# Load order, edge coefficients, late weights and pool waits in a fused grid, attention and MLP kernel

## The chip, the cores and the metric

The kernel runs on one core of a Trainium2 chip. The metric is device time in microseconds (us) of one execution; three runs are given and their median counts. The engines are TensorE (PE; its weight loads are PEld), VectorE (DVE), ScalarE (ACT), GpSimd (POOL) and SyncE (SP). SP only issues DMAs and reads registers. ACT and POOL issue DMAs as well; a DMA of SP or ACT is on a hardware queue, one of POOL on a software queue, and all of them use the same 16 DMA engines.

## The reference

The input x is (8, 512, 512) in f32. Four layers follow one another:

```python
# L0: one explicit step on a 512 x 512 grid, for each of the 8 batches
df = -(grad(A0*f, 1) + grad(A1*f, 2)) + 0.5*(grad2(B0*f, 1) + grad2(B1*f, 2)
      + grad(grad(B2*f, 2), 1) + grad(grad(B2*f, 1), 2))
x = maximum(f + df * dt, 0)             # one-sided differences in the outermost rows and columns
# L1: attention block with 16 heads, and an MLP
emb = silu(sin_emb(timestep)) @ W_ada + b_ada ; scale, shift = split(emb)
x = layernorm(x) * (1 + scale) + shift
q, k, v = x @ Wq + bq, x @ Wk + bk, x @ Wv + bv
probs = softmax(where(mask, -inf, q @ k.T / sqrt(32) + bias))
x = x + (probs @ v) @ Wo + bo
x = x + gelu2((layernorm(x) * g2 + beta2) @ W1 + b1) @ W2 + b2
# L2: an expert MLP chosen by an index per batch
x = layernorm(gelu(x @ Wi[e] + bi[e]) @ Wo_e[e] + bo[e] + x) * gamma[e] + beta[e]
# L3: a gated low-rank response
x = x + sigmoid(gate(mean(x))) * sigmoid(safety) * (x @ basis @ basis.T @ resp.T + resp_b + safety_bias)
```

The attention bias is (8, 16, 512, 512) in f32, 128 MB; it is the largest input. All matmuls are in f32.

## The kernel before

Three stages stand in the program one behind the other. `grid_stage` does L0 for batch 0 only, builds the grid's coefficient arrays and writes them to DRAM; I call it the front. `attention_stage` walks over 128 units (batch, group of four heads, quarter of the rows) and does the attention; in its gaps it also does the grid step of the next batches, from the coefficients in DRAM. `mlp_stage` does the two MLPs and L3, sixteen passes with the same matmul scheme. Nearly every instruction is pinned (`pin`, `tc.keep_in_program_order`), so each engine works through its list in the order of the program text. An instruction in the list that waits holds up all that is behind it on its engine; for SP and ACT this holds for DMA issues too. The hardware DMAs take eight completion semaphores in turn, POOL's DMAs eight others; a DMA may have to wait until the earlier one with the same semaphore has landed. I call this a slot wait.

**The embedding** (L104 to L139). ACT issues loads of ti (the time steps), freq, bada, sigs (the safety scores), eidx (the expert numbers), and later gw, dth, g2, beta2 and b1. DVE turns ti and freq into an angle ang; ACT takes Sin, Silu and, for sigs, Sigmoid, each with a table load of 1.28 us. This small work stands ahead of the front's large work on DVE. `embed` (L148) is 32 matmuls of 8 columns, each in two passes, into pe; `embed_out` (L157) adds bada and gives ada.

**The front's loads** (SP, L274). b1 and a1 in halves, b0, a0, the grid f, b2, 1 MB each as a whole; then wada in two halves of 1 MB, Wq, Wk, Wv, Wo (1 MB each), the rows of bq, bk, bv, and bo.

**The front's stencil.** DVE forms ca, cb, cc, ce, cg by sums of the raw arrays (ACT scales cc and b2), and then products with f: e, g, c, ga, gb, q, t. PE adds these up with shift matrices (L243), 28 matmuls of 512 columns in two passes each, into four PSUM banks acc. DVE forms x from acc row by row (L240), ACT takes the ReLU (L486).

**The edge rows.** Rows 0 and 511 of all batches need one-sided differences. They are done for all 8 batches together on 64 partitions: fe holds the edge rows of x, ec twelve coefficient rows, the same for every batch. POOL loads both behind an instruction gate_e that waits for f: for each of four column blocks one DMA of fe, and two of ec that read each DRAM row eight times. Some 23 DVE instructions (from qe on) make xe. Four DMAs of two pieces of 512 bytes put batch 0's edge rows from xe into x, two by SP and two by ACT (L492). POOL writes xe to DRAM as xed (L479), for the other batches.

**The coefficient writes.** Behind an instruction gate_c that waits for q, POOL issues writes of b2, ce, cc, cg, ca, cb to DRAM (coef_q, e, c, g, a, b; 1 MB each, and a few single rows).

**The front's end.** Statistics of x's rows (L499, L500), a power on POOL (L508), the scaling (L511), `embed_out`, and then in the attention stage the transposes xtr of x (`x1_in`) with scale and shift, pq and pk (the matmuls with Wq and Wk for the first head group), qt and kt, their evacuations by DVE and ACT, and the scores s. SP meanwhile reads the eight expert numbers from eidx (L1267), and then loads, in this order, mask mu, the grid gf of batch 1 (seven DMAs), gq (two halves of coef_q), the bias bt of unit 0, one half of coef_e (into xt of batch 1) and of coef_c, mask 1, the bias of unit 1, gg (half of coef_g), the bias of unit 2, and so on. POOL adds the mask to the bias (L950).

**Pools.** Each stage opens pools of tiles, and a new stage's tiles lie in memory that an older pool has given back. Without an option, the first use of such a tile waits until everything in the memory given back has been finished.

Of the kernel before, what the change touches and what calls it, by code (L numbers as in the profile page):

```python
# [11 lines left out]
F32 = mybir.dt.float32  # L12
# [8 lines left out]
NB = 8  # L21
# [18 lines left out]
def fused_kernel(ctx: ExitStack, tc: tile.TileContext, a: dict):  # L40
# [65 lines left out]
    nc.scalar.dma_start(freq, a["c_freq"])  # L106
    bada = ep.tile([P, 2 * KC], F32, name="bada")
    nc.scalar.dma_start(bada, a["b_ada"])
    nc.scalar.dma_start(sigs, a["safety"][None, :].to_broadcast([P, NB]))
    nc.scalar.dma_start(eidx, a["eidx"][None, :])  # L110
    nc.vector.tensor_scalar(bada[:, 0:KC], bada[:, 0:KC], 1.0, None, ALU.add)
# [27 lines left out]
    nc.scalar.activation(sigs, sigs, AF.Sigmoid)  # L139
# [14 lines left out]

    def embed_out(pe):
        tc.keep_in_program_order(
            nc.vector.tensor_tensor(  # L157
                ada, pe, bada[:, :, None].to_broadcast([P, 2 * KC, NB]), ALU.add
            )
        )  # L160
# [4 lines left out]
    def load_w():  # L165
        for n in ("Wq", "Wk", "Wv", "Wo"):
            w[n] = w8(wo8, n)
            nc.sync.dma_start(w[n], a[n].rearrange("(k p) m -> p k m", p=P))
# [5 lines left out]
    def load_rows():  # L174
        nc.sync.dma_start(bqk[:, 0, :], a["bq"])
# [6 lines left out]
        embed_out,  # L182
# [3 lines left out]
    io = ctx.enter_context(tc.tile_pool(name="io", bufs=1))  # L186
    g2 = const.tile([P, 2, KC], F32, name="g2")
    nc.scalar.dma_start(g2[:, 0, :], a["g2"])
    nc.scalar.dma_start(g2[:, 1, :], a["beta2"])
    b1 = const.tile([P, NJ], F32, name="b1")  # L190
    nc.scalar.dma_start(b1, a["b1"])
# [4 lines left out]
        g2, mhalf,  # L196
# [18 lines left out]
def grid_stage(  # L215
    tc, a, const, small, dram, x, mhalf, ident, load_wada, load_w, load_rows, embed,
    embed_out,
# [27 lines left out]
    with ExitStack() as ctx:  # L245
# [22 lines left out]
        pin(nc.gpsimd.memset(ec, 0.0))  # L268
# [7 lines left out]
        with tc.tile_pool(name="raw", bufs=1) as rp:  # L276
# [4 lines left out]
            def edge_in(i, k):  # L281
                lo, hi = max(0, W * k - 1), min(D, W * k + W + 1)
                u = slice(lo - W * k + 1, hi - W * k + 1)
                p0 = n * i
                pin(nc.gpsimd.dma_start(fe[p0 : p0 + n, :, u], a["edge_f"][:, :, lo:hi]))
                for side in range(2):
                    p1 = p0 + side * NB
                    pin(
                        nc.gpsimd.dma_start(
                            ec[p1 : p1 + NB, :, u],  # L290
                            a["edge_c"][side : side + 1, :, lo:hi].to_broadcast([NB, 12, hi - lo]),
                        )
                    )
# [9 lines left out]
            nc.scalar.dma_start(gw, a["c_ghost"].to_broadcast([P, 16]))  # L303
            nc.scalar.dma_start(dth, a["dt"][None, :].to_broadcast([P, NB]))
            load_wada()
            load_w()
# [6 lines left out]
            for i, k in enumerate(blocks):  # L313
                edge_in(i, k)
# [11 lines left out]
        wp = ctx.enter_context(tc.tile_pool(name="l0", bufs=1))  # L326
# [54 lines left out]
        for m, w, o in (  # L381
            ("q", b2, 1), ("e", ce, 1), ("c", cc, 0), ("g", cg, 1), ("a", ca, 0), ("b", cb, 0)
# [94 lines left out]
        xed = dram.tile([n, D], F32, name="xed")  # L477
        for i, k in enumerate(blocks):
            pin(nc.gpsimd.dma_start(xed[:, W * k : W * k + W], xe[n * i : n * i + n, :]))  # L479
        pe = embed(ps)  # L480
        pin(nc.vector.tensor_scalar(dth, dth, 0.5, None, ALU.mult))
        st = small.tile([P, R, 6], F32, name="ln0_st", tag="ln0_st", bufs=1)
        mv = small.tile([P, R, 2], F32, name="ln0_mv", tag="ln0_mv", bufs=1)
        for r in (0, 3, 1, 2):
            stt(x[:, r, :], acc[r], dth[:, 0:1], f[:, r, :], ALU.mult, ALU.add)
            pin(nc.scalar.activation(x[:, r, :], x[:, r, :], AF.Relu))  # L486
        for o, u, c in ((0, 3 * n, 0), (n, n, 2 * W)):
            for side, q_ in ((0, nc.sync), (1, nc.scalar)):
                p, r = side * (P - 1), side * (R - 1)
                e0 = o + side * NB  # L490
                pin(
                    q_.dma_start(  # L492
# [1331 lines left out]
```

## Time and profile before

| | us |
|---|---|
| runs (three) | 2828.27, 2830.43, 2831.24; median 2830.43 |
| profiled execution | 2828.87 |
| its span, first to last instruction | 2826.4 |
| PE busy | 2731.6 (97%) |
| DVE busy | 1942.6 (69%) |
| POOL busy | 1502.6 (53%) |
| ACT busy | 1003.3 (35%) |
| mean granted TensorE clock | 0.989 |
| chain that ended last, share of PE | 81% |

The page gives shares of the whole span; the front is some 70 us of it. Inside the front the timeline is the view to read: for each run of instructions its start, its length, engine, line, operation and tiles, and in brackets how long the engine had been idle and what released it. "SPq" and "ACTq" rows are DMA issues; a long one is an issue that was held up. The stretches table gives for each interval the busy time of each engine, the granted clock, and the share and rate of the DMA engines.

A few more rows of the front that the change touches, as start and length in us: the memset of ec on POOL 0.95, 1.39; the Sigmoid table load on ACT 7.70, 1.28; the first large DVE addition (ca) 11.05, 1.22; e on DVE 24.12, 2.29; the first stencil matmul on PE 26.51; fe and ec issues on POOL from 24.09 to 34.4, with 7.1 to 8.7 from issue to landing; qe on DVE 43.05, with 1.42 idle before it, for ec; xe's last instruction 51.82; gate_c on POOL 38.16; coef_b issued at 49.51 with 14.2 to landing; qt on DVE 77.06; gq on DVE from 77.72 (two in 4.28); the first softmax instruction on DVE 88.28.

### The profile page before, as it was taken

The page shows a single profiled execution, that of the slowest core. Times are in us where ns is not written, and L with a number is a line of the kernel's source. Part 1 is how long each engine was busy: PE and PEld are TensorE (multiplying, and loading weights), DVE is VectorE, ACT ScalarE, POOL GpSimd, SP SyncE. Part 2 cuts the span into 40 slices and gives each one's busy share as a digit, 9 for nine tenths or more (in the row PEclk, how much of TensorE's full clock was granted, in tenths as well). Part 3 has the DMA queues.
Part 4 walks back from the last instruction along what each step waited for, and adds up shares of the span by engine and source line. Part 5 has one row for each costly group of instructions (what it writes and reads, how often), then busy time and mean ns, then how long its engine had stood idle before and what let it go on. Part 6 is the DMA issues. An engine that isn't in the chain of part 4 may idle for free.

```text
span 2826.4 us, 39775 instructions
## 1 busy us (share of the span) xinstructions
PE 2731.6 (97%) x14646; PEld 2013.2 (71%) x14646; DVE 1942.6 (69%) x3583; ACT 1003.3 (35%) x2133; POOL 1502.6 (53%) x1080
## 2 busy tenths in 40 slices
PE   5999999999999998999999999999999999999997
PEld 3455555555555554888888888887888888888885
DVE  6889898888888766576756666655466565556654
ACT  1466666666666666211211211111121121121120
POOL 3455555555555553566555656564455455445532
PEclk9999999999999999999999999999999999999998
DMA  9665757666665554642444253343224233133110
GB/s 303 220 211 173 235 176 239 203 210 215 190 228 187 162 156 144 190 125 71 120 140 123 51 157 123 80 122 123 98 68 138 78 105 124 63 131 112 45 71 30
DMA packets 190399, 405.60 MB, mean 144 GB/s; under 512 B 24104, under 2 KB 28784, under 8 KB 183934
## 3 DMA queue, kind: packets, MB, share of 16 engines
q1 hardware_dynamic: 185192, 391.93, 41.8%
q0 software_dynamic: 3680, 11.07, 3.1%
q8 instruction: 116, 1.90, 0.3%
q14 instruction: 77, 0.63, 0.1%
q10 hardware_dynamic: 1334, 0.07, 0.0%
HBM read 367.32 MB, written 31.50 MB: 141 GB/s over the span
## 4 chain that ended last, share of the span: by engine, by line
PE 81%; DVE 13%; ACT 2%; issue 1%; POOL 0%; DVEq 0%; POOLq 0%; ACTq 0%
PE u L1137 27%; PE y L1137 24%; PE tr L546 6%; PE s L543 4%; PE ctx L543 4%; PE o L543 3%; PE pv L543 3%; PE pq L543 3%; PE pk L543 2%; DVE bt L973 2%; DVE tb L1143 2%; DVE x L663 1%; DVE pt L998 1%; ACT bt L978 1%; DVE act L1143 1%
## 5 line engine op out<-in xcount | busy, mean ns | idle before, releaser
L1137 PE MATMUL y<-wo,act 128*128 128x256 f32 x2560 | 578.9, 381 | 0.0
L950 POOL TENSOR_TENSOR bt<-bt,mk 128x1024 f32<-128x1024 f32 x256 | 543.2, 2143 | 63.8 <-DMA bt<-in_bias 62.9
L1137 PEld LDWEIGHTS y<-wo,act 128*128 128x128 f32 x2560 | 479.3, 190 | 82.2 <-issue 20.5
L978 ACT ACTIVATE bt<-bt,mn 128x512 f32<-128x512 f32 x512 | 365.5, 715 | 116.3 <-DVE mn L973 116.2
L546 PEld LDWEIGHTS tr<-ident,bt 128*128 128x128 f32 x2048 | 228.1, 141 | 168.8 <-issue 115.5
L1137 PE MATMUL u<-bt,wi 128*128 128x256 f32 x1440 | 332.4, 381 | 0.0
L973 DVE CUSTOM_DVE_ANT_0 bt<-s,bt 128x512 f32<-128x512 f32 x512 | 330.4, 683 | 0.0
L1143 DVE TENSOR_TENSOR act<-u,u 128x512 f32<-128x512 f32 x256 | 173.4, 687 | 212.8 <-PE u L1137 138.0
L1137 PEld LDWEIGHTS u<-bt,wi 128*128 128x128 f32 x1440 | 274.6, 191 | 37.6
L546 PE MATMUL tr<-ident,bt 128*128 128x128 f32 x2048 | 280.0, 278 | 19.3 <-DVE pt L998 8.1
L998 DVE COPY pt<-tr 128x512 f32<-128x512 f32 x256 | 175.9, 687 | 110.6 <-PE tr L546 110.3
L1137 PE MATMUL u<-tb,ws 128*128 128x256 f32 x1024 | 242.3, 379 | 0.0
L1137 PE MATMUL y<-t,s 128*128 128x256 f32 x1024 | 234.1, 380 | 0.0
L1137 PEld LDWEIGHTS u<-tb,ws 128*128 128x128 f32 x1024 | 195.0, 190 | 26.7
L1000 ACT COPY pt<-tr 128x512 f32<-128x512 f32 x256 | 148.3, 579 | 180.1 <-PE tr L546 177.7
L1146 POOL TENSOR_TENSOR t<-wo,t 128x512 f32<-128x512 f32 x64 | 104.6, 1650 | 198.2 <-PE y L1137 198.2
L1137 PEld LDWEIGHTS y<-t,s 128*128 128x128 f32 x1024 | 190.6, 190 | 23.8
L1143 DVE TENSOR_TENSOR x<-y,x 128x512 f32<-128x512 f32 x96 | 64.6, 686 | 182.5 <-PE y L1137 128.5
L1449 ACT ACTIVATE act<-act,bi 128x512 f32<-128x512 f32 x128 | 83.9, 712 | 292.2 <-DVE act L1143 292.1
L1449 ACT ACTIVATE act<-act,b 128x512 f32<-128x512 f32 x128 | 82.9, 712 | 292.5 <-DVE act L1143 292.5
L543 PE MATMUL s<-kt,qt 32*128 32x512 f32 x1024 | 170.8, 643 | 2.1 <-DVE mn L973 1.1
L1143 DVE TENSOR_TENSOR u<-u,u 128x512 f32<-128x512 f32 x192 | 131.3, 684 | 59.5 <-PE u L1137 59.5
(313 smaller groups left out, 4282.4 us busy)
## 6 DMA issues: line engine op xcount, KB each, us to landing
bt<-in_bias SPq DMA_DIRECT2D x256, 512.0 KB
wo<-in_W SPq DMA_DIRECT2D x32, 1024.0 KB
wi<-in_Wi SPq DMA_DIRECT2D x32, 1024.0 KB
wo<-in_Wo_e SPq DMA_DIRECT2D x32, 1024.0 KB
wi<-in_W SPq DMA_DIRECT2D x28, 1024.0 KB
gq<-coef_q SPq DMA_DIRECT2D x21, 512.0 KB
x1d<-x SPq DMA_DIRECT2D x8, 1024.0 KB
x<-x1d SPq DMA_DIRECT2D x8, 1024.0 KB
```

Of the source, the lines that this page charges most:

```text
L543: pin(nc.tensor.matmul(out, lhsT=lhsT, rhs=rhs, start=start, stop=stop))
L546: pin(nc.tensor.transpose(out, src, ident))
L663: pin(nc.vector.tensor_tensor(out, x, y, op))
L950: nc.gpsimd.tensor_tensor(bt, bt, mask[b, r][:, None, :].to_broadcast([P, 2, S]), ALU.add)
L973: nc.vector.tensor_tensor_reduce(bt[:, i, :], ss[h], bt[:, i, :], -1.0, 3.0e38, ALU.add, ALU.min, mn)
L978: nc.scalar.activation(bt[:, i, :], bt[:, i, :], AF.Exp, bias=mn, scale=-1.0, accum_out=sums[b, c, r][:, h : h + 1],)
L998: pin(nc.vector.tensor_copy(pt[:, :, r % 2, :], tr))
L1000: pin(nc.scalar.copy(pt[:, :, r % 2, :], tr))
L1137: pin(nc.tensor.matmul(out, lhsT=lhsT, rhs=rhs, start=start, stop=stop))
L1143: pin(nc.vector.tensor_tensor(out, x, y, op))
L1146: pin(nc.gpsimd.tensor_tensor(out, x, y, op))
L1449: nc.scalar.activation(acts[g][:, k, :], acts[g][:, k, :], func, bias=bi[:, j : j + 1])
```

## The change

It has these parts. Line numbers in the diff are left out.

- **Start.** bada, eidx, gw, dth, g2, beta2 and b1 are no longer loaded by ACT. sigs is loaded by SP as its first DMA and its Sigmoid comes first on ACT. gw and dth come behind b2 on SP; bada and eidx behind Wk; g2, beta2 and b1 behind the mask loads in the attention stage. The addition of 1 to bada's first half moves behind xe on DVE.
- **Edge coefficients.** Each coefficient row is loaded once, to a tile ec8 of 8 partitions, at the start and by POOL. A tile sel8 made from the identity spreads each of the 8 partitions to the 8 batches by four matmuls of 390 columns, first in PE's list; ACT copies the results to ec, ahead of its scaling of cc. Only fe stays behind gate_e.
- **Edge rows and xed.** The four edge DMAs are issued after the ReLU of rows 0 and 3, ahead of that of rows 1 and 2. The xed writes go from POOL to ACT, behind the ReLUs.
- **Late weights.** Wv is loaded behind the bias of unit 0, Wo behind that of unit 1.
- **Waits.** The pools l0, io, aw, ap, a_ps, fw, fa and f_ps are opened with `reuse_waits="tile"`: a tile waits for what its own memory held.
- **Orders.** coef_g is written ahead of coef_c. `grid_early(0)`, the two products of gq with the grid of batch 1, moves from behind the first pq to ahead of it; on DVE they then stand before qt.

```diff
+    nc.sync.dma_start(sigs, a["safety"][None, :].to_broadcast([P, NB]))
+    nc.scalar.activation(sigs, sigs, AF.Sigmoid)
     bada = ep.tile([P, 2 * KC], F32, name="bada")
-    nc.scalar.dma_start(bada, a["b_ada"])
-    nc.scalar.dma_start(sigs, a["safety"][None, :].to_broadcast([P, NB]))
-    nc.scalar.dma_start(eidx, a["eidx"][None, :])
-    nc.vector.tensor_scalar(bada[:, 0:KC], bada[:, 0:KC], 1.0, None, ALU.add)
...
-    nc.scalar.activation(sigs, sigs, AF.Sigmoid)
...
     def load_rows():
+        nc.sync.dma_start(bada, a["b_ada"])
+        nc.sync.dma_start(eidx, a["eidx"][None, :])
...
-    io = ctx.enter_context(tc.tile_pool(name="io", bufs=1))
+    io = ctx.enter_context(tc.tile_pool(name="io", bufs=1, reuse_waits="tile"))
...
-            def edge_in(i, k):
-                lo, hi = max(0, W * k - 1), min(D, W * k + W + 1)
-                u = slice(lo - W * k + 1, hi - W * k + 1)
-                p0 = n * i
-                pin(nc.gpsimd.dma_start(fe[p0 : p0 + n, :, u], a["edge_f"][:, :, lo:hi]))
-                for side in range(2):
-                    p1 = p0 + side * NB
-                    pin(
-                        nc.gpsimd.dma_start(
-                            ec[p1 : p1 + NB, :, u],
-                            a["edge_c"][side : side + 1, :, lo:hi].to_broadcast([NB, 12, hi - lo]),
-                        )
-                    )
+            ec8 = rp.tile([N // NB, 12, W + 2], F32, name="ec8")
+            sel8 = rp.tile([N // NB, N // NB, NB], F32, name="sel8")
+            pin(nc.gpsimd.memset(ec8, 0.0))
+            for i, k in enumerate(blocks):
+                c, u = edge_cols(k)
+                pin(nc.gpsimd.dma_start(ec8[2 * i : 2 * i + 2, :, u], a["edge_c"][:, :, c]))
+            pin(
+                nc.gpsimd.tensor_copy(
+                    sel8, ident[0 : N // NB, 0 : N // NB, None].to_broadcast([N // NB, N // NB, NB])
+                )
+            )
...
-            nc.scalar.dma_start(gw, a["c_ghost"].to_broadcast([P, 16]))
-            nc.scalar.dma_start(dth, a["dt"][None, :].to_broadcast([P, NB]))
+            nc.sync.dma_start(gw, a["c_ghost"].to_broadcast([P, 16]))
+            nc.sync.dma_start(dth, a["dt"][None, :].to_broadcast([P, NB]))
             load_wada()
-            load_w()
+            load_w("Wq", "Wk")
             load_rows()
...
-                edge_in(i, k)
+                c, u = edge_cols(k)
+                pin(nc.gpsimd.dma_start(fe[n * i : n * i + n, :, u], a["edge_f"][:, :, c]))
+
+            for i in range(4):
+                pec = ps.tile([N, 3, W + 2], F32, name=f"pec_{i}", tag="pec", bufs=2)
+                mm(
+                    pec, sel8.rearrange("q s b -> q (s b)"), ec8[:, 3 * i : 3 * i + 3, :],
+                    True, True,
+                )
+                pin(nc.scalar.copy(ec[:, 3 * i : 3 * i + 3, :], pec))
...
-            ("q", b2, 1), ("e", ce, 1), ("c", cc, 0), ("g", cg, 1), ("a", ca, 0), ("b", cb, 0)
+            ("q", b2, 1), ("e", ce, 1), ("g", cg, 1), ("c", cc, 0), ("a", ca, 0), ("b", cb, 0)
...
         for r in (0, 3, 1, 2):
             stt(x[:, r, :], acc[r], dth[:, 0:1], f[:, r, :], ALU.mult, ALU.add)
             pin(nc.scalar.activation(x[:, r, :], x[:, r, :], AF.Relu))
+            if r == 3:
+                edges()
+        xed = dram.tile([n, D], F32, name="xed")
+        for i, k in enumerate(blocks):
+            pin(nc.scalar.dma_start(xed[:, W * k : W * k + W], xe[n * i : n * i + n, :]))
...
         load_bias(*units[0])
+        load_w("Wv")
         grid_loads(1, -1)
         mask_in(0, 1)
         load_bias(*units[1])
+        load_w("Wo")
         for c in range(KC):
             x1_in(0, c)
+        grid_early(0)
         mask_out(0, 0)
         pin(nc.scalar.copy(bvr, bvc[:, :, None].to_broadcast([P, KC, P])))
         add_mask(*units[0])
         drain(q_block(0, 0))
-        grid_early(0)
         grid_early(1)
         drain(k_block(0, 0, "ctx"))
         mask_out(0, 1)
         load_bias(*units[2])
         mask_in(0, 2)
         mask_in(0, 3)
+        load_late()
```

## The prediction

> **What bounds the kernel now.** First the page's overview: TensorE has nearly no idle slice, except in the first two of 40.
>
> ```profile
> span 2826.4 us, 39775 instructions
> PE   5999999999999998999999999999999999999997
> ```
>
> Each slice is 70.7 us, so all of the change's room, one boundary apart, is ahead of about 100 us. Next, the table of 10 us stretches. Its columns are the stretch, its length, busy us of PE, PEld, DVE, ACT and POOL, granted clock, DMA share and GB/s.
>
> ```profile
> 20.00:30.00 10.00, 3.49 (x4) 1.52 (x5) 9.96 (x5) 3.21 (x2) 6.94 (x10) 1.00 1.04 372
> ...
> 50.00:60.00 10.00, 10.00 (x59) 8.09 (x57) 6.29 (x16) 2.52 (x4) 6.04 (x23) 0.88 1.03 418
> 60.00:70.00 10.00, 4.43 (x22) 4.37 (x22) 3.95 (x11) 0.00 (x0) 1.05 (x1) 0.50 0.67 231
> 70.00:80.00 10.00, 10.00 (x28) 5.51 (x26) 4.47 (x5) 2.58 (x4) 1.95 (x1) 0.77 1.03 360
> 80.00:90.00 10.00, 9.22 (x28) 3.84 (x27) 9.93 (x17) 3.58 (x6) 5.59 (x4) 1.00 0.83 320
> ```
>
> Four limits follow one another: VectorE (DVE) and the loads that feed it up to 26 us; PE without a gap to 63 us; nobody from 63 to 69; then DMA (share 1.03) and DVE. The timeline says what the gap waits for:
>
> ```profile
> 39.48 14.11 SPq L178 DMA_DIRECT2D bo<-in_bo  x1
> ...
> 53.37 9.85 PE L148 MATMUL pe<-sc,wada 128*128 128x8 f32 x64
> ...
> 55.06 6.78 ACTq L492 DMA_DIRECT2D x<-xe  x2
> ...
> 60.42 1.38 SPq L492 DMA_DIRECT2D x<-xe  x2
> 63.55 0.70 DVE L499 BATCH_NORM_STATS2 ln_st<-x 128x6 f32<-128x512 f32 x1 [6.84 <-DMA x<-xe]
> ...
> 68.79 3.64 PE L546 MATMUL xtr<-ident,x 128*128 128x128 f32 x16 [5.57 <-DVE ada L157]
> ```
>
> The edge rows xe were computed by 52.04, but their four tiny DMAs leave late: SP is held in the issue of bo for 14.11 us (I read this as a queue full of Wq to Wo), then reads eight expert numbers until 60.1; ACT's two wait for the queue slots of Wv and Wo. So the layernorm's last statistics start at 63.55 and PE stands still for 5.57 us.
>
> **The change, part by part.**
>
> *Start.* ca is DVE's first large addition; it started at 11.05, held by the embedding's small work: Sin ran at 10.51 because ACT first issued five small DMAs, two with waits, and loaded its tables at 7.70. Now ti and freq alone stay on ACT and sigs goes ahead on SP (its issue took 0.77 us). The angle is ready at 9.03 (DVE) and the Sin table then already loaded: Sin 9.1, ca 9.65, a gain of 1.4. Behind it DVE waited 1.11, 0.18 and 0.23 for a and b, 1.5 in all. SP's third load used to issue at 5.81 behind a slot; now five large ones go at once. The 6.3 MB at the trace's 0.42 MB/us from about 3 us bring a0 by 14.5 and f by 17, ahead of DVE's need (16.7 and 21.2). So e starts at 24.12-2.9 = 21.2 and PE's stencil at 26.51-2.9 = 23.6. From there PE has no gap: its embed matmuls start at 50.5 and end at 60.3.
>
> *Edge coefficients.* Eight broadcast DMAs (0.58 us of POOL each, 8.0 to 8.7 to landing) go; four of 24 rows come at once after a small memset, issued about 3.3 to 5.5, landed about 14. Four matmuls over 390 columns follow: the cold 512-column pass took 0.86, so 8 passes x 0.66 = 5.3 us, PE idle otherwise, done by 20. Four ACT copies (512 columns take 0.59, so 0.45 each) stand ahead of the scaling of cc, which may end at 22.4; DVE wants cc at 25.6. Cover: 3 us; past that each us late costs one. (ga, wanted at 27.8, takes ec8's memory and now waits for the same spread; all of DVE and then PE stand behind it, with 7 us of cover.) The fe loads follow f, land about 30 and are wanted at 38.7, so qe's wait of 1.42 goes, and xe is ready at 52.04-2.9-1.4 = 47.7.
>
> A rule applies here. Cold passes at the stencil's start took 0.86 against 0.43 later: 5.52 us for eight against 3.60, 1.9 lost. The Trainium skill, "TensorE: Matmul & The Clock Gate" (Part 1), has the clock rise after about 3.4 us of work and fall after an idle window of that length. The new matmuls end some 3.6 us ahead of the stencil: by the rule it may start warm and PE gains 10.4 in place of 8.5; by the row nothing. I take the row; the load chain below decides in both cases.
>
> *Edge rows early, late weights behind.* Ahead of the edge rows stand 6.3 MB of front loads, 4.2 of wada, Wq, Wk and 0.3 of bo: 10.8 MB, about 30 us, so SP's queue is empty and the expert numbers read before 49. Both queues issue after two ReLUs: the r0 and r3 updates wait for PE (47.9 and 48.8), ACT ends at 50.3, the DMAs are out by 51.1. Landing took under 2 us after the last issue at 61.8; I say 53.3. ACT does its other two ReLUs behind the issues, to 52.4; xed's four issues follow there (2 us), with nothing for ACT until 61. In the trace 63.55 to 68.47 is 4.9 us of statistics, POOL's power and scaling: now 53.5 to 58.4, hidden under embed to 60.3 with 1.9 to spare. So xtr starts at 60.3, not 68.79: **PE is 8.5 us ahead** (2.9 + 5.57). The moved add on bada (0.16) is hidden too. What is late next is embed itself.
>
> *Waits tile by tile.* The mask load waited for everything in the front's pools, last for xed (64.59). It now waits for coef_a and coef_b, whose memory it takes. gate_c lets the six 1 MB coefficient writes go at 35.2 instead of 38.2, onto an empty DMA. Their rate alone on POOL's queue is not in the trace. The mixed row (404 to 438 GB/s, 48 to 60 us) gives 15.5 us and an end at 53.5. The Trainium skill, "DMA: Bandwidth & Descriptors" (Bandwidth), gives 341 GB/s for a 1 MB transfer from GpSimd: an estimated 18.4 us, end 56.5. Its Specifications also set 358 GB/s as the HBM limit, which this trace exceeds. I take 53.5 from the row; the other end is the range's.
>
> From the mask load on SP's order is as before (mask, gf, gq, bt, e, c), 64.59-53.5 = 11.1 earlier, but Wv (1.05 MB, 2.7 us at 0.39 MB/us) now stands ahead of e, and Wo behind bt 1. Before, gq landed about 10 us behind the mask load: now 63.5. DVE multiplies it before qt, not after: 63.9 to 66.3, while PE does pq until 77.03-8.5 = 68.5. So qt loses nothing and gq's time (4.28, slowed by POOL's adds) leaves the path. Next on DVE is the e product, at 81.93 before. Its data, 5.3 MB behind the mask load, come at 71.4; it then starts 10.5 earlier, and 1.2 more is won if POOL's adds (67 to 73) slow it less. The first softmax goes from 88.28 to about 77. PE's second pq can end at 99.7-8.5 = 91.2; qt of c=1, at 103.47 before, comes at 92.4. **From there all moves by 11 us**: later loads wait for buffers that DVE frees, so they move with it.
>
> *MLP boundary.* PE stood 0.88 us between o and u, behind DVE x L655 (the whole pool's release); tile-wise only about 0.1 is left: -0.8. The weights landed long before.
>
> Sum: 11.0 + 0.8 = 11.8. The profiled execution took 2828.87 (span 2826.4), so 2817.1; the median shown is 2830.43, 1.6 above it: **2818.6**.
>
> **Rivals.**
>
> *Loads set the pace (2823).* The coefficient writes reach only 340 GB/s (-3), and Wo ahead of gg costs part of its 2.7: gain 11.8-3-1.5 = 7.3. For: DMA share 1.03 from 70 to 80, and 4 MB of loads that PE waits on follow. Against: DVE needs gg only 12 us after e.
>
> *Given back (2828).* The 2.1 MB moved behind the edges are paid twice: 5.4 us in the DMA-bound stretch, and first-batch DVE (9.9 of 10 from 80 to 120) waits for each load. 11-5.4-3 leaves under 3. For: share and DVE rows. Against: Wv and Wo are used only from 82 and 113.
>
> *Tile waits do little.* The last of a set of waits is all that counts: coef_b landed at 63.7, the mask load went at 64.6. Were SP's queue not emptied, 0.9 us would be won there and 2.9 at the start: 2826.
>
> *Slower (2835).* gq now stands before qt on DVE: if it lands late, qt, the scores and PE wait behind it. qt is later than before once gq lands past 77.06-2.4 = 74.6, that is with the mask load at 64.6, or coefficient writes that take 29 us (220 GB/s). At 185 GB/s (34 us) qt comes at 82.8: 5.7 late, less the boundary's 0.8. For: from 30 to 38 us the trace shows 161 to 198 GB/s at full DMA share. Against: there the small broadcast rows of ec and fe ran, mostly gone now, and the writes themselves ran above 400.
>
> **How the numbers follow.** My forecast 0.60 (own range 2814 to 2821.5, from coef end 51.5 to 56.5 and the 1.9 of a warm start); load-paced 0.20; given back or tile waits alone 0.14; slower 0.06. A change under 0.2% (5.7 us) can't be told from none: faster is 0.60 + 0.19, same 0.15, slower 0.06. Eight in ten lie from 2812.5 to 2825.5.
>
> **What would show it.** Right: e's product on DVE near 21.2, embed ending near 60.3 with xtr directly behind it, the mask load near 53.5, the first softmax near 77. Wrong: a DVE wait at gq or e after 66 for its DMA (load-paced), PE idle between embed and xtr (edge rows still late), a wait at c or PE's stencil behind the coefficient copies, or a first softmax 11 us earlier whose gain is gone by 200 us (given back).

## The result, and the profile after

| kernel | runs | median us | lowest to highest | time over before, 95% interval |
|---|---|---|---|---|
| before | 7 | 2829.87 | 2827.60 to 2831.24 | |
| changed | 7 | 2817.53 | 2815.82 to 2820.80 | 0.9960 (0.9949 to 0.9972) |

The change saves 12.3 us by the medians, with an interval of some 8 to 14 us; 2818.6 was forecast. The profiled execution of the changed kernel took 2819.7 us, with a span of 2817.8 (8.6 less than before) and a mean granted clock of 0.991. The page's overview has, for the two lines shown of before:

```profile
span 2817.8 us, 39784 instructions
...
PE   7899999999999998999999999999999999999997
```

PE's first slice has gone from 5 tenths to 7. The table of 10 us stretches (columns as before: stretch, length, busy us of PE, PEld, DVE, ACT and POOL, granted clock, DMA share, GB/s) shows where:

```profile
20.00:30.00 10.00, 6.94 (x10) 3.01 (x11) 9.97 (x6) 2.78 (x2) 2.71 (x5) 1.00 1.05 355
30.00:40.00 10.00, 10.00 (x31) 4.96 (x30) 9.62 (x23) 0.17 (x1) 4.58 (x10) 1.00 0.68 237
...
50.00:60.00 10.00, 10.00 (x69) 9.42 (x68) 6.95 (x17) 1.78 (x3) 1.05 (x1) 0.81 0.73 246
60.00:70.00 10.00, 10.00 (x32) 5.94 (x30) 4.91 (x7) 2.58 (x4) 2.37 (x2) 0.85 0.87 296
70.00:80.00 10.00, 9.22 (x28) 4.03 (x28) 7.20 (x20) 4.70 (x9) 4.31 (x4) 1.00 1.05 410
```

PE is now busy through the stretch from 60 to 70 us, where it had 4.43. DVE isn't: from 70 to 80 it works 7.20 us of 10, while the DMA stands at full share. Before 40 us there is something new: a DMA share of 0.68. The timeline of the changed kernel, by engine and in order of time (start, length, engine, line, operation; in brackets the idle time before it and what ended it), has these lines in the place of those shown of before:

```profile
27.81 1.32 SPq L184 DMA_DIRECT2D bo<-in_bo  x1
...
50.02 1.65 SPq L507 DMA_DIRECT2D x<-xe  x2
...
50.89 1.81 ACTq L507 DMA_DIRECT2D x<-xe  x2
50.96 8.89 PE L145 MATMUL pe<-sc,wada 128*128 128x8 f32 x64
...
59.70 3.55 PE L570 MATMUL xtr<-ident,x 128*128 128x128 f32 x16
```

The issue of bo takes 1.32 us, not 14.11; the edge rows go out 10.4 us earlier on SP; PE's xtr stands directly behind embed, 9.1 us earlier. Further on, the loads of batch 1's grid on SP's queue. Before (timeline of SP):

```profile
64.59 0.34 SPq L564 DMA_DIRECT2D mu<-in_mask  x1
...
68.16 2.36 SPq L680 DMA_DIRECT2D gq<-coef_q  x2
```

In the changed kernel:

```profile
52.85 0.34 SPq L588 DMA_DIRECT2D mu<-in_mask  x1
...
54.81 0.77 SPq L713 DMA_DIRECT2D gf<-in_x  x1
56.30 0.32 SPq L714 DMA_DIRECT2D gf<-in_x  x1
58.87 0.22 SPq L715 DMA_DIRECT2D gf<-in_x  x1
59.75 0.22 SPq L716 DMA_DIRECT2D gf<-in_x  x1
60.02 0.83 SPq L704 DMA_DIRECT2D gq<-coef_q  x2
```

The waits of its SP queue from 48 to 75 us (line, what it waited for, us in total, times, longest) have among them:

```profile
SPq L715 <- DMA xed<-xe: 2.2, 1, 2.2
...
SPq L588 <- DMA x<-xe: 1.0, 1, 1.0
...
SPq L714 <- DMA xed<-xe: 0.7, 1, 0.7
SPq L716 <- DMA xed<-xe: 0.6, 1, 0.6
```

And what DVE does with the loads:

```profile
64.28 2.50 DVE L687 TENSOR_TENSOR gq<-gq,gf 128x1024 f32<-128x1024 f32 x2 [0.93 <-DMA gq<-coef_q]
66.72 0.75 DVE L641 TENSOR_SCALAR qt<-pq,bqk 128x512 f32<-128x512 f32 x1
72.73 1.22 DVE L687 TENSOR_TENSOR x<-x,gf 128x1024 f32<-128x1024 f32 x1 [5.26 <-DMA x<-coef_e]
```

The mask load goes at 52.85, 11.7 us earlier than before. Its last wait is for an edge row (`x<-xe`). But from there to the issue of gq are 7.2 us, where before they were 3.6: three of gf's seven loads (L714 to L716) stand in the queue, and what each waits for is a write of xed. DVE waits 5.26 us for the half of coef_e.

One mark is used from here on: **the start of qt of c=1**, on DVE. Before and changed:

```profile
103.47 0.75 DVE L617 TENSOR_SCALAR qt<-pq,bqk 128x512 f32<-128x512 f32 x1
...
92.35 0.74 DVE L641 TENSOR_SCALAR qt<-pq,bqk 128x512 f32<-128x512 f32 x1
```

It lies behind all that the change touches in the front and, in nearly all these kernels, ahead of the stretches where the granted clock dips (see the end). Its 11.1 us are what the front gained. 3.0 us of them are lost on the way to the MLP, 2.6 of these across two dips of the granted clock; 0.6 are won at the boundary.

### The profile page after: what moved, and what is told of

It is laid out like the page before. It is cut to its first block, busy times and chain, and to the rows that moved or that the text cites. A ratio compares the mean times of both kernels' runs of the same rounds, so it can differ in the third digit from the quotient of the medians.

```text
span 2817.8 us, 39784 instructions
## 1 busy us (share of the span) xinstructions
PE 2737.7 (97%) x14654; PEld 2014.0 (71%) x14654; DVE 1939.5 (69%) x3583; ACT 1004.6 (36%) x2137; POOL 1497.0 (53%) x1073
## 4 chain that ended last, share of the span: by engine, by line
PE 82%; DVE 13%; ACT 2%; issue 1%; DMA 1%; SPq 0%; POOL 0%; ACTq 0%; DVEq 0%; POOLq 0%
PE u L1164 27%; PE y L1164 24%; PE tr L570 6%; PE s L567 4%; PE ctx L567 4%; PE o L567 3%; PE pv L567 3%; PE pq L567 3%; PE pk L567 2%; DVE bt L997 2%; DVE tb L1170 2%; DVE x L687 2%; DVE pt L1022 1%; ACT bt L1002 1%; DVE act L1170 1%
```

## The experiments

Twelve kernels were run, each against the kernel before on the same chip. The intervals are some 0.12% to each side, or 3 us, so kernels between 2815 and 2821 can't be told apart by their times alone. The traces tell more: qt of c=1 is given for each. One profiled execution stands for each kernel. How far the mark varies between executions of one kernel is not on record; the seven kernels with the same start have e's product at 20.57 to 20.81, so a difference of 0.3 us is hardly more than chance.

| kernel | median us | time over before, 95% interval | qt of c=1, us |
|---|---|---|---|
| before | 2829.3 to 2830.5 | | 103.47 |
| changed | 2817.53 | 0.9960 (0.9949 to 0.9972) | 92.35 |
| start_only | 2831.92 | 1.0008 (1.0001 to 1.0014) | 104.32 |
| start_bada | 2827.41 | 0.9995 (0.9987 to 1.0004) | 100.64 |
| start_late | 2820.59 | 0.9970 (0.9957 to 0.9982) | 94.52 |
| start_spread | 2820.96 | 0.9969 (0.9958 to 0.9979) | 94.65 |
| pool_waits | 2821.55 | 0.9970 (0.9961 to 0.9979) | 93.43 |
| ec_dma | 2819.93 | 0.9971 (0.9958 to 0.9983) | 93.54 |
| gq_late | 2818.06 | 0.9956 (0.9940 to 0.9971) | 92.68 |
| weights_front | 2817.33 | 0.9954 (0.9939 to 0.9969) | 91.61 |
| xed_pool | 2815.35 | 0.9952 (0.9937 to 0.9967) | 90.51 |
| both | 2816.15 | 0.9949 (0.9935 to 0.9962) | 90.46 |
| xed_wv | 2815.25 | 0.9955 (0.9938 to 0.9971) | 90.68 |
| ec_dma_xed | 2818.94 | 0.9963 (0.9950 to 0.9977) | 93.38 |

### Which part pays: parts of the change on the kernel before

**start_only.** The new order of the first small loads alone: below, and as in the change gw and dth behind b2, and g2, beta2 and b1 behind the mask loads, all on SP's queue.

```diff
     nc.scalar.dma_start(freq, a["c_freq"])
+    nc.sync.dma_start(sigs, a["safety"][None, :].to_broadcast([P, NB]))
+    nc.scalar.activation(sigs, sigs, AF.Sigmoid)
     bada = ep.tile([P, 2 * KC], F32, name="bada")
-    nc.scalar.dma_start(bada, a["b_ada"])
-    nc.scalar.dma_start(sigs, a["safety"][None, :].to_broadcast([P, NB]))
-    nc.scalar.dma_start(eidx, a["eidx"][None, :])
...
     def load_rows():
+        nc.sync.dma_start(bada, a["b_ada"])
+        nc.sync.dma_start(eidx, a["eidx"][None, :])
...
```

> The kernel before with one part of the change: the small loads of the first microseconds in the new order (table loaded early, ti and freq alone on ScalarE's queue, rows and late vectors on SP's). Edge coefficients, late weights, edge rows, xed and all pool waits as before. Theory A (the edge rows' queue sets the end of the front): e at 20.6, stencil at 23.1, embed ends near 60, but PE then stands idle until the edge rows land; xtr at 66 to 68 instead of 59.7, mask load at 62 to 64, time gains at most 3 us: 2827.5 to 2830. Rival B (the start's 3 us carry through to the end with little idle and the rest is the tile waits'): xtr at 62 to 64, time 2824 to 2826.

Measured: 2831.92, which is slower than before. e comes at 19.78, 4.3 us earlier, and PE's embed ends at 58.9. Theory A had the direction, PE idle for the edge rows, but not the size: xtr comes at 70.51, 1.7 later than before. The timeline of start_only:

```profile
26.04 12.49 SPq L179 DMA_DIRECT2D bada<-in_b_ada  x1
...
45.52 10.12 SPq L184 DMA_DIRECT2D bo<-in_bo  x1
...
59.67 0.17 DVE L154 TENSOR_SCALAR bada<-bada 128x4 f32<-128x4 f32 x1 [13.08 <-DMA bada<-in_b_ada]
...
70.51 3.65 PE L555 MATMUL xtr<-ident,x 128*128 128x128 f32 x16 [11.60 <-DVE ada L159]
```

SP's queue is full, and b_ada now lies in it behind the weights. DVE's small addition waits 13.08 us for it, the row updates stand behind that addition, and PE then idles for 11.60 us, twice as long as before. A start that is 4 us earlier is worth nothing while the queue that feeds the end of the front is not.

**start_bada.** As start_only, with b_ada back on ACT's queue.

```diff
     bada = ep.tile([P, 2 * KC], F32, name="bada")
+    nc.scalar.dma_start(bada, a["b_ada"])
...
     def load_rows():
-        nc.sync.dma_start(bada, a["b_ada"])
```

> The kernel before with the new order of the first small loads, but b_ada loaded early on ScalarE's queue as before; weights in front, broadcasts, edges, xed and waits as before. Theory A (in the new order alone it was b_ada behind the weights that stopped VectorE's row updates until 60.0; behind that, SP's queue with bo's issue until 55.6): row updates at 47 to 50, edge rows on SP at 55.7 to 58, xtr at 61 to 65, time 2822 to 2827. Rival B (b_ada is a symptom; the edge rows and the expert numbers still wait for the whole queue): edge rows on SP at 60 or later, xtr at 67 or later, 2828 or more.

Measured: 2827.41, between the two theories. The rows' statistics start at 50.71, so b_ada did hold up DVE; the issue of bo still takes 9.85 us (until 50.6), the edge rows leave at 57.61 on SP and at 59.71 on ACT, and xtr comes at 67.06 after 7.91 us of idle PE. So 3.5 us of the 70.51 were b_ada's, and the larger part is the full queue.

**start_late and start_spread.** start_only with one more part of the change each: Wv and Wo loaded in the attention stage, or the edge coefficients spread by TensorE.

start_late:

```diff
-            load_w()
+            load_w("Wq", "Wk")
...
         load_bias(*units[0])
+        load_w("Wv")
         grid_loads(1, -1)
         mask_in(0, 1)
         load_bias(*units[1])
+        load_w("Wo")
```

start_spread (with ec8, its four loads and sel8 ahead of the large loads, as in the change):

```diff
-                edge_in(i, k)
+                c, u = edge_cols(k)
+                pin(nc.gpsimd.dma_start(fe[n * i : n * i + n, :, u], a["edge_f"][:, :, c]))
+            for i in range(4):
+                pec = ps.tile([N, 3, W + 2], F32, name=f"pec_{i}", tag="pec", bufs=2)
...
+                pin(nc.scalar.copy(ec[:, 3 * i : 3 * i + 3, :], pec))
```

> The kernel before with two parts of the change: the new order of the first small loads, and Wv and Wo loaded in the attention stage. Edge coefficients by broadcast DMA, edge rows behind all ReLUs, xed on POOL and whole-pool waits as before. With the new order alone, b_ada lay on SP's queue behind Wv and Wo, landed at 59.7, and VectorE and then PE (11.6 us) stood for it: slower than before. Theory A (what has to be cleared is SP's queue ahead of the small rows; late weights or fewer broadcast bytes each clear it): e at 19.8, VectorE's add on b_ada without a wait before 50, edge rows out by 56, xtr at 60 to 63, mask load 54 to 58, first softmax 78 to 80, time 2820 to 2824. Rival B (only both together clear it): xtr at 66 or later, 2826 or more.

> The kernel before with two parts of the change: the new order of the first small loads, and the edge coefficients spread by TensorE. Wv and Wo in front, edge rows behind all ReLUs, xed on POOL and whole-pool waits as before. Theory A (as for late weights: without the eight broadcasts the DMA has 360 GB/s or more in place of 164 to 170 from 30 to 36 us, so the queue empties in time): e at 20.6, b_ada landed before 46, xtr at 60 to 63, mask load 54 to 58, first softmax 78 to 80, time 2820 to 2824. Rival B: xtr at 66 or later, 2826 or more.

Measured: 2820.59 and 2820.96, mask load at 56.16 and 56.41. PE, start_late and then start_spread:

```profile
60.14 3.65 PE L555 MATMUL xtr<-ident,x 128*128 128x128 f32 x16 [1.38 <-issue]
...
60.72 3.65 PE L566 MATMUL xtr<-ident,x 128*128 128x128 f32 x16 [0.88 <-issue]
```

Theory A holds for both, and this is the main finding: **either part alone clears the queue**. With neither the kernel is 2 us slower than before, with one of them about 9 us faster. Windows of 4 us show how (columns as above). start_only:

```profile
28.00:32.00 4.00, 4.00 (x11) 1.85 (x10) 4.00 (x9) 0.00 (x0) 0.63 (x2) 1.00 1.07 296
32.00:36.00 4.00, 4.00 (x16) 2.25 (x16) 3.90 (x4) 0.17 (x1) 1.83 (x5) 1.00 1.05 170
```

start_spread:

```profile
28.00:32.00 4.00, 4.00 (x11) 1.84 (x10) 4.00 (x5) 0.00 (x0) 0.00 (x0) 1.00 1.04 387
32.00:36.00 4.00, 4.00 (x13) 1.86 (x12) 3.90 (x9) 0.00 (x0) 0.87 (x3) 1.00 1.04 387
```

At the same full share the DMA moves 170 GB/s while the last of the eight broadcasts are in flight (issued by 28.7, with a median of 8.1 us to landing) and 387 without them. The small loads of fe are in flight in start_only too; in start_spread, where they are alone from 24 to 28, the DMA moves about 300. That clears the queue by rate; late weights clear it by 2.1 MB less ahead of b_ada, and in start_late the slow stretch is still there (182 GB/s from 32 to 36).

### What the pair does together, and the tile waits

**weights_front.** The changed kernel with Wv and Wo loaded in the front.

```diff
-            load_w("Wq", "Wk")
+            load_w("Wq", "Wk", "Wv", "Wo")
...
-        load_w("Wv")
...
-        load_w("Wo")
```

> The changed kernel with one part undone: Wv and Wo are loaded again in the front, behind Wk. Theory A (the loads behind the mask load set the pace; late weights cost more than they give): in the changed kernel the DMA engines are partly idle from 28 to 36 us (share 0.68 from 30 to 40), so Wv and Wo fit there. The edge DMAs still go at about 50 us, the mask load at about 53, xtr starts at 59.7 as before; coef_e lands some 2.6 us earlier, its product on DVE starts at about 70 in place of 72.7, the first softmax at about 74.5 in place of 77.2, qt of c=1 at about 89.8 in place of 92.4, where PE's second pq ends. Time 2 to 3 us under the changed kernel's. Theory B (the prediction's: the weights in front of the edge rows held the queue): SP is held in the issue of bo or in the slot waits until past 53, the edge rows land at 56 or later, xtr starts at 62 or later, and the time is 2 us or more above the changed kernel's.

Measured: 2817.33, qt of c=1 at 91.61. The prediction's reason for late weights falls: the edge rows are not held (SP at 49.17), xtr comes at 59.67, and the DMA is at share 1.05 from 32 to 36 where the changed kernel has 0.24: there was room for the 2.1 MB. Theory A holds for the queue but not for the time: coef_e's product starts at 70.38 as it expected, but takes 2.83 us, and of the 2 to 3 us only 0.7 are left at the mark. These 0.7 need not be the late weights' own price: with the mask load at 54.47 none of gf's loads stands for xed here, and with xed's writes out of the way (both against xed_pool, below) the difference is gone. Late weights, once the spread is there, clear nothing.

**ec_dma.** The changed kernel with the broadcasts back.

```diff
-                c, u = edge_cols(k)
-                pin(nc.gpsimd.dma_start(fe[n * i : n * i + n, :, u], a["edge_f"][:, :, c]))
-            for i in range(4):
-                pec = ps.tile([N, 3, W + 2], F32, name=f"pec_{i}", tag="pec", bufs=2)
...
-                pin(nc.scalar.copy(ec[:, 3 * i : 3 * i + 3, :], pec))
+                edge_in(i, k)
```

> The changed kernel with the edge coefficients fetched again by eight broadcast DMAs behind f, as before; no memory rows of eight, no matmuls, no copies. Theory A: ec lands near 36 to 39; DMA at full share with 160 to 240 GB/s from 30 to 38; qe on DVE waits 1 to 2 us, which PE hides; the coefficient writes end 1 to 3 us later and with them the mask load (54 to 56); gq's loads go when the gf slots and the mask allow, 60 to 62; first softmax 77 to 79, time 0 to 2 us above the changed kernel (2817.5 to 2819.5): spreading by TensorE is worth little by itself. Stencil start 23.06 within 0.3 (the copies of the changed kernel delay nothing). Rival B (the early copies on ScalarE and the eight matmuls pay: they let the front's DVE run through): e or stencil 1 us or more apart, time 3 us or more above.

Measured: 2819.93, qt of c=1 at 93.54, 1.2 later than with the spread. Theory A holds, a little above its range in time, except for the start: e comes at 19.78, not 20.62. So the spread has a price in the front. DVE's waits of 0.42 and 0.20 for b and a, and f's arrival 1.25 us later (gate_e at 18.62, against 17.37), are there only with the four early loads. It wins this back behind the front. On SP's queue gq is issued at 60.02 with the spread and at 61.17 with the broadcasts, where ACT issues the last two writes of xed only at 54.75 (53.84 with the spread) and gf's last two loads stand for them. The coefficient writes are faster with the spread, too: coef_b lands at 53.1 (issued at 40.38, 12.7 to landing) instead of 54.6 (42.88 and 11.7), although e came 0.8 us later. With the broadcasts, POOL's issue of coef_a stands 3.73 us for coef_q; with the spread 0.39.

**pool_waits.** The changed kernel without the pool option: below, and so for aw, ap, a_ps, fw, fa and f_ps.

```diff
-    io = ctx.enter_context(tc.tile_pool(name="io", bufs=1, reuse_waits="tile"))
+    io = ctx.enter_context(tc.tile_pool(name="io", bufs=1))
...
-        wp = ctx.enter_context(tc.tile_pool(name="l0", bufs=1, reuse_waits="tile"))
+        wp = ctx.enter_context(tc.tile_pool(name="l0", bufs=1))
...
```

> The changed kernel with the waits of its pools for the whole earlier pool again, as before; all else as changed. Theory A (tile waits matter, since the coefficient loads' memory is freed one tensor at a time): the mask load waits for everything of the front's pools, the xed writes last, so it goes at 58 or later instead of 52.85; gq's products end past 69 and qt of c=0 comes after them; first softmax 81 to 83 instead of 77.2, qt of c=1 97 to 98; PE stands again 0.6 to 0.9 us between o and u in the MLP. Time 5 to 6 us above the changed kernel, 2823. Rival B (the last of a set of waits is all that counts, xed at 54.7 plus landing): mask load by 56, softmax within 1.5 of the changed kernel's, time 2818 to 2819.

Measured: 2821.55, inside neither theory whole. The mask load goes at 56.04 (B), the first softmax at 78.23 (B), qt of c=1 at 93.43: 1.1 later, not 5. The time is 4.0 above the changed kernel, but by the trace 1.1 of this is the front, 0.6 the MLP, and the rest of the profiled difference (3.8) arises where the clock dips (0.76 and 0.81 from 108 to 116 us, where the changed kernel has 1.00, and one more near the end of the attention). The eleven executions keep the difference (2819.63 to 2823.50, against 2815.82 to 2820.80 of the changed kernel), so it is not the chance of one; why this kernel should have more dips is not shown. The boundary is plain. Timeline of PE, pool_waits:

```profile
1136.78 3.69 PE L1164 MATMUL u<-hT,w 128*128 128x256 f32 x16 [0.88 <-DVE x L679]
```

and the changed kernel, where u follows o without a gap:

```profile
1125.83 6.60 PE L567 MATMUL o<-Wo,ct 128*128 128x512 f32 x15
1132.27 3.62 PE L1164 MATMUL u<-hT,w 128*128 128x256 f32 x16
```

The mask load's 3.2 us of lead come to 1.1, for a reason that can be read from two issues: pool_waits issues gq at 59.61, the changed kernel at 60.02. The lead was gone by then, lost to the slots of xed; only gf's first megabyte had come earlier. What the tile waits are worth once xed is out of the way (xed_pool, below) was not run; there gq is issued at 56.05, so it may be more than 1.1.

**gq_late.** gq's products behind qt again.

```diff
-        grid_early(0)
         mask_out(0, 0)
...
         drain(q_block(0, 0))
+        grid_early(0)
```

> The changed kernel with one part undone: the two products of gq stand behind qt on DVE again. Theory A: DVE waits 5.26 us for coef_e behind qt in the changed kernel, so the two products (2.5 us) fall into that wait: coef_e's product at 72.7, first softmax at 77.2, time the changed kernel's within 1 us. Theory B (the prediction's step: the products leave DVE's path): the first softmax comes 2.4 to 4.3 us later, at 79.6 or later, and the time is some 2 to 4 us above.

Measured: 2818.06, qt of c=1 at 92.68. The timeline of DVE, gq_late:

```profile
66.81 0.75 DVE L641 TENSOR_SCALAR qt<-pq,bqk 128x512 f32<-128x512 f32 x1 [3.63 <-PE pq L567]
67.47 5.68 DVE L687 TENSOR_TENSOR gq<-gq,gf 128x1024 f32<-128x1024 f32 x2
73.07 1.21 DVE L687 TENSOR_TENSOR x<-x,gf 128x1024 f32<-128x1024 f32 x1
```

The two products take 5.68 us beside POOL's additions and still end within 0.4 us of coef_e's arrival (72.73 in the changed kernel). The order is worth 0.3 us at most, because what was taken off DVE's path was lying beside a wait for the DMA.

### The new limit: small writes ahead of large loads

**xed_pool.** The changed kernel with xed's four writes on POOL's queue, right behind xe, as before.

```diff
+        xed = dram.tile([n, D], F32, name="xed")
+        for i, k in enumerate(blocks):
+            pin(nc.gpsimd.dma_start(xed[:, W * k : W * k + W], xe[n * i : n * i + n, :]))
         pe = embed(ps)
...
-        xed = dram.tile([n, D], F32, name="xed")
-        for i, k in enumerate(blocks):
-            pin(nc.scalar.dma_start(xed[:, W * k : W * k + W], xe[n * i : n * i + n, :]))
```

> The changed kernel with one part undone: the four xed writes are issued by POOL again, right behind xe. Theory A (slot waits): in the changed kernel two of the loads of gf waited on SP at 56 to 59 us for the slots that the xed writes on ACT's queue hold, so that gq was issued at 60.0, 7.2 us behind the mask load, where the kernel before took 3.6. With xed on POOL gq goes at about 56.5, the product with coef_e starts at about 69.5 in place of 72.7, qt of c=1 at about 89.8 (PE's limit) in place of 92.4: 2 to 3 us under the changed kernel's time. Theory B (the DMA engines are the limit there, not the issue): gq is issued earlier but coef_e lands at 72 all the same, and the time is the changed kernel's within 1 us.

Measured: 2815.35, the mark at 90.51; Theory A holds. Timeline of SP's queue, xed_pool:

```profile
51.68 0.49 SPq L588 DMA_DIRECT2D mu<-in_mask  x1
...
55.75 0.25 SPq L716 DMA_DIRECT2D gf<-in_x  x1
56.05 1.97 SPq L704 DMA_DIRECT2D gq<-coef_q  x2
```

gf's loads go through, gq is issued 4.0 us earlier. That it was the slot and not gf's memory is seen in the changed kernel itself: the first of the seven loads writes the same tile and went at 53.37, while the writes of xed were still being issued (52.80 to 54.7); only later loads stood. The count fits the slots: from the first write of xed on, the ninth DMA of SP and ACT is gf's fourth load, and the three behind it are those that stood. In ec_dma only gf's last two loads stand (3.1 and 0.9 us), and there only the last two writes of xed went late. So SP's and ACT's DMAs share the eight slots, and four small writes on ACT hold up SP. DVE, xed_pool:

```profile
63.19 2.35 DVE L687 TENSOR_TENSOR gq<-gq,gf 128x1024 f32<-128x1024 f32 x2
67.80 0.75 DVE L641 TENSOR_SCALAR qt<-pq,bqk 128x512 f32<-128x512 f32 x1 [2.26 <-PE pq L567]
...
90.51 0.75 DVE L641 TENSOR_SCALAR qt<-pq,bqk 128x512 f32<-128x512 f32 x1 [1.35 <-PE pq L567]
```

Now DVE waits for PE at both qt, and for coef_e only 0.74 us: loads have all but stopped setting the pace here.

**both** (weights_front and xed_pool together) and **xed_wv** (xed_pool, with Wv's load behind coef_e and coef_c) try to win more from the loads.

```diff
-        load_w("Wv")
         grid_loads(1, -1)
+        load_w("Wv")
```

> The changed kernel with Wv and Wo in the front and the xed writes on POOL. Theory A: coef_e lands some 5 to 6 us earlier than in the changed kernel, by 67.5; its product follows qt almost directly, the first softmax comes at about 72.5 to 73, and now PE (second pq, ends at about 89.4) sets qt of c=1, at about 89.5. So the gain over the changed kernel is about 3 us, not the 5 that the loads win: 2814.5, 15.4 under the kernel before. Theory B: each of the two parts gives under 1 us, and both together stay within 1.5 us of the changed kernel.

> The changed kernel with two changes: xed's four writes on POOL's queue right behind xe, and Wv's load behind that of e's coefficients instead of ahead. Theory A (with the gf slots free early, PE's first and second pq set the pace, not loads): e product directly behind qt of c=0 with under 0.3 us wait (0.74 with xed moved alone), first softmax 73 to 74, qt of c=1 at 90.3 to 90.6 behind PE's pq, so no gain at the end over xed moved alone: 2814.8 to 2816. Rival B (loads still set it): qt of c=1 at 89.5 or earlier and 2814 or less.

Measured: 2816.15 and 2815.25, the mark at 90.46 and 90.68 against 90.51. Neither wins anything over xed_pool; in xed_wv e's product stands directly behind qt (68.63), and qt of c=1 again waits 1.30 for PE. In these two kernels PE is the bound up to the mark.

**ec_dma_xed.** xed_pool with the broadcasts back: it should keep the 0.8 us of the earlier stencil.

```diff
+                edge_in(i, k)
...
+            pin(nc.gpsimd.dma_start(xed[:, W * k : W * k + W], xe[n * i : n * i + n, :]))
...
-            pin(nc.scalar.dma_start(xed[:, W * k : W * k + W], xe[n * i : n * i + n, :]))
```

> The changed kernel with the edge coefficients by eight broadcast DMAs and xed's four writes on POOL's queue right behind xe. Theory A (with the gf slots free PE sets the pace, and PE starts the stencil 0.8 us earlier without the spread): e at 19.8, xtr at 58.8 to 59, mask load at 52.5 to 53.8, qt of c=0 at 66.8 to 67.3 behind PE's pq, first softmax 73 to 74, qt of c=1 at 89.5 to 90; time 2814 to 2815. Rival B (the coefficient writes, slowed by the broadcasts, set it through the mask load): gq or e waits more than 1 us for its DMA, first softmax 75 or later, time 2816 to 2818.

Measured: 2818.94, the mark at 93.38. Rival B holds, 0.9 above its range in time. xtr does come at 58.87, but gf's second load stands until 55.14, DVE waits 2.66 for the second half of gq and 5.09 for coef_e, and the first softmax is at 78.19. The profile puts gf's wait down to the load of bvc, which had been issued by 31; coef_b fits better, since it was issued at 42.95 with 11.8 to landing, that is 54.75, but the mask load had not stood for it (51.46), and in both the same load of gf went at 53.04, with coef_b landing at 55.0. This wait is left open. With the xed writes out of the way the spread is worth 2.9 us at the mark, where it was worth 1.2 with them in the way.

xed_pool, both and xed_wv are the fastest kernels of this case. Their intervals overlap with that of the changed kernel; that they are faster rests on the traces, where the mark is 1.7 to 1.9 us earlier for a reason that is visible.

## Why the prediction was right, and where it wasn't

The total (12.3 against 11.8) and the chain of places held. That the two totals lie within 0.5 us is luck: the interval runs from 8 to 14 us, and the two profiled executions differ by 8.6 us of span. There the 11.0 us of the front and the boundary came nearly as forecast (11.1 and 0.6), and 3.0 us were lost between them, which the forecast put at nothing. Its parts, by their steps:

*Start.* Held in size: ca at 8.55 (forecast 9.65, the Sin table load begins at 3.59), waits for b and a of 0.62 in place of the 1.5 before, e at 20.62 against 21.2, the stencil at 23.06 against 23.6. What failed is the reading of it as a gain of its own, 2.9 us to be added: start_only has all of it and is slower than before.

*Edge coefficients.* The matmuls took 5.43 us (5.3), the copies 0.48 each (0.45), both hidden. The choice of the row, a cold stencil, was right: its first eight passes took 6.56 us, colder still than the 5.52 before (the clock column says 1.00 there in both; the passes tell otherwise). PE stood 4.52 us ahead of it, not the 3.6 expected; both are longer than the window of about 3.4 us of the Trainium skill ("TensorE: Matmul & The Clock Gate", Part 1), so the rule, too, allowed a cold start. The cost at nothing was wrong by the 0.8 us that e came later than with the broadcasts. The part's value was set too low: it was only given the wait at qe, though the slow stretch was seen (it stands under the slower rival).

*Edge rows early, late weights behind.* Edge rows at 50.0 to 52.7 and xtr at 59.70 against 60.3: held. But the layernorm's path from the edge rows took 6.6 us (53.40 to 60.0), not 4.9: the statistics of all four rows stand behind the ReLUs of rows 1 and 2, and these behind ACT's edge DMAs. Of the 1.9 us of cover nearly nothing was left; embed ended at 59.85. The working counts 10.8 MB ahead of the edge rows; it was right that the queue would be empty, but it gave this to the late weights. weights_front, start_late and start_spread show that late weights and spread do the same work, and that the second of them adds nothing here. Issuing the edge rows ahead of two ReLUs was not run alone: start_late, with all ReLUs first, has xtr at 60.14 after 1.38 us of idle PE.

*Tile waits.* The mask load came at 52.85 (53.5), but not for the reason given. coef_b, the last of the 6.3 MB, landed at 53.1, behind the mask load, and in gq_late at 54.5 with the mask load at 52.86; so the mask load did not wait for it. What it waited for last was an edge row (1.0 us), and that the two times agree is luck. The landing itself was forecast well, by a sum that doesn't close: 15.5 us from 35.2 give 50.7, not 53.5, and the 2.8 us between have no name. coef_b landed 17.9 us after the first issue, waits included. The estimate from the 341 GB/s of the Trainium skill ("DMA: Bandwidth & Descriptors", Bandwidth), 18.4 us, lies nearer to that than 15.5, although the rate was above it while the writes ran (398, 414 and 399 GB/s from 40 to 52 us, with other traffic). "From the mask load on SP's order is as before" was true of SP's list and failed for the slots: xed's move to ACT put four writes into the rotation that gf's loads take over. From mask load to gq 7.2 us, not 3.6; coef_e at 72.7, not 71.4. That "gq's time (4.28) leaves the path" failed as well: it is worth 0.3. Both errors lie in the same stretch, and neither moved the sum. The first softmax (77.16, forecast 77) and the mark (92.35, forecast 92.4) came out of the one wait for coef_e: its product started 1.3 late, but ran in 1.22 us, since POOL's additions (67.63 to 71.8) were over, and the first softmax followed 4.4 us behind its start, where the forecast had 5.6. That these two errors cancel is luck.

*MLP boundary.* 0.6 of the 0.8: the gap of 0.88 is closed wholly, measured where the shift of all later work changes from 8.1 to 8.7.

*From there all moves by 11.* This step failed: the shift is 11.3 us at 146 us, 9.9 from 311, 8.1 at 1108, and 8.7 behind the boundary. It isn't given back to loads, as the rival would have it, but lost for the most part where the clock dips (below), which the working has no term for. The load-paced rival was true for one product: a wait of DVE for e's data after 66 was to be a sign of it, and DVE waited for them until 72.73; xed_pool, which ends this wait, has the mark 1.8 us earlier. But the forecast itself had these data at 71.4. "Tile waits do little" was near the truth in the front as the change has it (1.1 of the 11 us are theirs), though not for the whole change, and gq ahead of qt didn't hold it up: pq ended at 66.69, and qt started at 66.72.

## What to carry to other kernels

Parts of a change can be substitutes: price each with the others absent, and with them present, before adding. A cleared queue counts by what it carries last, so a small row must not be moved behind megabytes, and a start made earlier is worth nothing until the queue's end is. When a DMA moves to another queue, look at who inherits its completion slot as well as at who is queued behind it.

## What the runs showed of the hardware that was not expected

The granted clock dips for some microseconds at nearly the same places of the work in all fourteen traces, among them one between 135 and 160 us and one between 1071 and 1092. By the traces' clock records it is at half in a dip, for 3.4, 6.8 or 10.2 us. Windows of 10 us of the changed kernel:

```profile
130.00:140.00 10.00, 7.26 (x41) 4.37 (x39) 9.05 (x21) 7.60 (x18) 3.79 (x4) 0.91 0.52 156
140.00:150.00 10.00, 9.38 (x56) 5.00 (x57) 6.18 (x14) 4.39 (x11) 6.16 (x5) 0.58 0.58 189
```

and of 4 us near the end of the attention:

```profile
1074.00:1078.00 4.00, 4.00 (x27) 1.31 (x29) 0.00 (x0) 1.41 (x4) 4.00 (x3) 0.50 0.29 111
```

Before has the same dips, shorter (0.67 from 150 to 160, 0.70 from 1086 to 1090). Of the changed kernel's front gain 1.1 us go between 146 and 182 and 1.5 between 1078 and 1108. In xed_pool's trace the second dip is shorter than in the changed kernel's (0.77 and 0.80 from 1070 to 1078), and its span, 2813.0, is 13.4 under that of before. These two dips follow stretches with gaps in PE (7.26 of 10 above), but other such stretches have none behind them (7.12 of 10 from 90 to 100 in the changed kernel). What sets a dip off was not tried, and a profile of one execution can't say whether a kernel has it always.

In all fourteen traces the clock falls to half some 4 to 5 us after the start of the embed matmuls, and the stage of PE that follows them starts at it: 0.52 and 0.62 from 56 to 64 us in the changed kernel, 0.50 in weights_front and ec_dma, though PE is busy without a gap. Those matmuls have 8 columns, and PEld is busy as long as PE (4.00 of 4.00 from 56 to 60 in the changed kernel, at a clock of 0.52). Busy by the table, they don't keep the clock up.

Tiny DMAs can be slow to finish among large ones. In the changed kernel xed's four writes (8 KB each) were issued by 54.7, behind gf's first megabyte (53.37), and the last of the slots they held came free at 59.75, while the DMA moved 319 GB/s from 56 to 60. In weights_front they were issued by 54.8, ahead of that megabyte (54.99), and no load of gf stood for them.
